# Two graph layers around an eigenvalue problem: one ScalarE table load, the first pair normed by batch, layer-0 work on both sides of a branch, a shorter norm

## The chip, the cores and the metric

The kernel runs on one core of one Trainium2 chip. The core has five engines that run on their own and meet at semaphores: TensorE (PE, matrix products into PSUM), ScalarE (ACT, functions and copies), VectorE (DVE, elementwise work and sums), GpSimd (POOL) and SyncE (SP), which here issues all the DMAs. The metric is the device time of one execution in microseconds, the lower the better.

## The reference

`x` is 64 matrices of 256 x 256 in float32. The result goes through two layers, each with a layer norm, a ReLU and a residual. Layer 0 multiplies by the squared adjacency matrix `adj * adj` three times, with weights of 256 x 512, 512 x 1024 and 1024 x 256. Layer 1 multiplies by the eigenvectors of a normalized Laplacian of the adjacency matrix.

```python
h = jnp.maximum(_layernorm(x, axis=-1), 0.0)
x = x + _L0_gnn_ref(h, adj, adj, W1, W2, W3)      # relu((adj*adj) @ (h @ W)), the last without relu
h = jnp.maximum(_layernorm(x, axis=-1), 0.0)
x = x + _L1_gnn_ref(h, adj, L1_W1, L1_b1, L1_W2, L1_b2)

# in _L1_gnn_ref
deg = jnp.sum(A, axis=0) + jnp.sum(A, axis=1) - jnp.diagonal(A)
L_norm = d_inv_sqrt[:, None] * (jnp.diag(deg) - A) * d_inv_sqrt[None, :]
_, U = jnp.linalg.eigh(L_norm)
agg = jnp.einsum('mn,bnd->bmd', U.T, features)
h = jax.nn.relu(agg @ W1 + b1)
return jnp.einsum('nm,bmd->bnd', U, h @ W2 + b2)
```

## The kernel before

There are two strands of work. The first is the eigenvalue problem, in the class `Eigen`: `laplacian` builds the matrix, `tridiagonalize` reduces it with 254 reflections, `leaves` solves blocks of 16 by steps on DVE, `level` merges blocks to 32, 64, 128 and 256, and `vectors` ends with the eigenvectors `u`, their transpose `ut`, and a flag that says whether anything went wrong on the quick way. This is a long chain of short instructions, most of them on DVE. In each reflection PE transposes two columns into rows (`psB`, `psA`), so DVE waits for PE and PE for DVE.

The second strand is layer 0 and the first half of layer 1, in the class `Layers`. It takes the 64 matrices in 32 pairs. `begin` loads a pair (`load`), norms it and writes `h0`; `first` multiplies by the squared adjacency `gt2`, `second` by W1 and `gt2`, `third` by W2, `fourth` by W3 in two halves, `last` by `gt2` and adds the residual to give `x1`. Then `norm1`, `turn_rows` and `for_layer1` give `hw`. `x1` and `hw` of all pairs but the last two are put into DRAM. Both strands need PE and ACT.

`Pace` sets the order in which the two strands stand on PE and ACT. It is written out while the program is built: `Pace` keeps a clock for each engine and a cost for each operation. `chain` issues an operation of the eigenvalue strand and, before it, lets `run` issue what the two generators of `Layers` (`products` and `rows`) have to offer and what by these costs can start earlier. Within an engine everything then runs in that order. For a small DVE operation the cost is 0.065 us plus one 960th of a microsecond for each element.

At the end of the eigenvalue strand `tile_kernel` calls `pace.go_on(FLAG_US)`, which issues so much more PE work by the planner's clock, and then `mend`. `mend` loads the flag into a register on every engine and branches: if the flag is set, the eigenvalues are done again by a slow way (with these inputs it is not set, and the branch jumps over that code). After it all engines meet. Then `layer1` fetches `hw` and `x1` of the first three pairs from DRAM (`fetch`), and in a loop over 32 pairs runs `to_vectors`, `from_vectors` and `finish`, in three stages that overlap. What is left of the second strand is mixed in until `pace.finish()` at turn 8.

The order at the front: SP issues `adj`, `ident`, `lower`, the two halves of the first pair (by rows, `h`), then the weights and the rest. The layer norm is in `norm`: four sums on ACT, the mean `nm` on DVE, four sums of squares on ACT, the variance `v`, a square root on ACT, one refining step of it on DVE, the reciprocal `scale` and the product `shift`; `relu_norm` then applies both with four ACT instructions. The profile's lines are nearly all line 191, in `issue`, since `Pace` makes the calls there; so one goes by the names of tiles.

Of the kernel before, what the change touches and what calls it, by code (L numbers as in the profile page):

```python
# [29 lines left out]
H = 2  # L30
PAIRS = 32
KEPT = 2
LAST_AT = 12
FLAG_US = 6.0
LN_EPS = 1e-5
EPS = 2.0**-24
BIG = 1.0e3
# [213 lines left out]
class Eigen:  # L251


    def __init__(self, tc, ctx, ap, gt2, pace):
        self.tc, self.nc, self.pace = tc, pace.now, pace
        self.gt2 = gt2
        self.ap = ap
        pool = ctx.enter_context(tc.tile_pool(name="eig_const", bufs=1))
        dma = tc.nc.sync.dma_start
        self.adj = pool.tile([P, H, N], F32, name="adj")  # L260
        dma(out=self.adj, in_=ap["adj"].rearrange("(h p) n -> p h n", p=P))
        mats = [pool.tile([P, H, N], F32, name=c) for c in ("ident", "lower", "upinc", "sub")]
        self.mats = mats
        self.ident, self.lower, self.upinc, self.sub = mats
        self.load_matrices(0, 2)
        self.iota, self.far, self.ones = (pool.tile([P, N], F32, name=c) for c in ("iota", "far", "ones"))
        tc.nc.vector.memset(self.ones, 1.0)
        self.cols = pool.tile([P, 1 + len(LEVELS), H], F32, name="cols")
        self.leaf = pool.tile([P, LEAF + 2], F32, name="leaf")
        self.mp = ctx.enter_context(tc.tile_pool(name="eig_mat", bufs=1))  # L270
        self.sp = ctx.enter_context(tc.tile_pool(name="eig_small", bufs=2))
        self.lp = ctx.enter_context(tc.tile_pool(name="eig_leaf", bufs=1))
        self.ps = ctx.enter_context(tc.tile_pool(name="eig_psum", bufs=1, space=PSUM))
# [1428 lines left out]
class Layers:  # L1702


    def __init__(self, tc, ctx, ap, gt2, u, ut):
        self.tc, self.nc, self.ap = tc, tc.nc, ap
        self.gt2, self.u, self.ut = gt2, u, ut
        pool = ctx.enter_context(tc.tile_pool(name="layers", bufs=1))
        self.kept = ctx.enter_context(tc.tile_pool(name="kept", bufs=KEPT))
        dram = ctx.enter_context(tc.tile_pool(name="dram", bufs=1, space=bass.MemoryType.DRAM))  # L1710
        self.x1, self.hw = {}, {}
        self.x, self.h0, self.y1, self.y2, self.s2, self.p3, self.h1, self.new = ({} for _ in range(8))
        self.begun = set()
# [24 lines left out]

    def load(self, q):
        self.x[q] = x = self.io.tile([P, H, 2, N], F32, tag="x", name="x")  # L1740
        for h in range(H):
            yield self.nc.sync.dma_start(out=x[:, h], in_=self.view(self.ap["x"], q)[:, h])

    def open(self, ctx):

# [29 lines left out]
        for i, (lhsT, rhs) in enumerate(pairs):  # L1775
            yield self.nc.tensor.matmul(out, lhsT=lhsT, rhs=rhs, start=i == 0, stop=i == len(pairs) - 1)

    def norm(self, x, scale, shift):

        nc = self.nc  # L1780
        g = H * 2
        s, nm, v, tmp = (self.sp.tile([P, g], F32, tag=c, name=c) for c in ("s", "nm", "v", "tmp"))
        for j in range(g):
            junk = self.sp.tile([P, N], F32, tag="junk", name="junk", bufs=1)
            yield nc.scalar.activation(junk, x[:, j // 2, j % 2, :], AF.Copy, accum_out=s[:, j : j + 1])
        yield nc.vector.tensor_scalar(nm, s, -1.0 / N, None, OP.mult)
        for j in range(g):
            junk = self.sp.tile([P, N], F32, tag="junk", name="junk", bufs=1)
            yield nc.scalar.activation(
                junk, x[:, j // 2, j % 2, :], AF.Square, bias=nm[:, j : j + 1], accum_out=v[:, j : j + 1]  # L1790
            )
        yield nc.vector.tensor_scalar(v, v, 1.0 / N, LN_EPS, OP.mult, OP.add)

        yield nc.scalar.activation(s, v, AF.Sqrt)
        yield nc.vector.reciprocal(tmp, s)
        yield nc.vector.tensor_tensor(tmp, tmp, v, OP.mult)
        yield nc.vector.tensor_tensor(s, s, tmp, OP.add)
        yield nc.vector.tensor_scalar(s, s, 0.5, None, OP.mult)
        yield nc.vector.reciprocal(scale, s)
        yield nc.vector.tensor_tensor(shift, nm, scale, OP.mult)  # L1800

    def relu_norm(self, x, scale, shift, tag):
        h = self.wp.tile([P, H, 2, N], F32, tag=tag, name=tag)
        for j in range(H * 2):
# [4 lines left out]
        return h  # L1809

    def project(self, rows, blocks, rhs, tag):

        out = self.wp.tile([P, blocks, 2 * N], F32, tag=tag, name=tag)
        for c in range(blocks):
            ps = self.bank()
            for b in range(2):
                yield from self.products_of(
                    ps[:, b * N : (b + 1) * N],
                    [(rows[:, h, b, c * P : (c + 1) * P], rhs[:, h, :]) for h in range(H)],
                )  # L1820
            yield self.nc.scalar.copy(out[:, c, :], ps)
        return out

    def streams(self):
        return Stream(self.products()), Stream(self.rows())
# [1 line left out]
    def products(self):  # L1827


        yield lambda: 0 in self.h0  # L1830
        yield from self.first(0)
        yield from self.second(0)
        for q in range(PAIRS):
# [6 lines left out]
            if q > 0:  # L1840
                yield from self.for_layer1(q - 1)
            if more:
                yield lambda: q + 1 in self.h0
                yield from self.first(q + 1)
            yield from self.fourth(q, 1)
            if more:
# [17 lines left out]
    def begin(self, q):  # L1864
# [73 lines left out]
    def norm1(self, q):  # L1938
# [4 lines left out]
        h1 = yield from self.relu_norm(x1, scale, shift, "h1")  # L1943
        self.h1[q] = h1

    def turn_rows(self, q):
# [100 lines left out]
    def layer1(self, pace):  # L2047
# [29 lines left out]
def tile_kernel(ctx: ExitStack, tc: tile.TileContext, ap):  # L2077
# [5 lines left out]
    with ExitStack() as inner:  # L2083
# [52 lines left out]
```

## Time and profile before

| | us |
|---|---|
| median of 3 runs | 2467.62 (2467.04 to 2468.11) |
| the profiled execution | 2468.13 |
| its span, from the first to the last instruction | 2466.3 |
| mean granted TensorE clock | 0.998 of full speed |
| ACT busy | 1011.8 |
| PE waits on `xr` of DVE | 69 times |
| the 64 loads of the input, from issue to landing | 3.7 (median) |

The chain of work that ended last goes back only to 2271.93, to SP's issue of the first fetch after the branch:

```profile
2271.93 0.02 SPq L191
2271.95 0.03 issue
2271.98 0.03 SPq L191
2272.01 0.04 issue
2272.05 3.01 DMA hw<-hw
2275.07 0.97 issue
2276.03 53.67 PE bank L191 x243
```

The columns are the start in us, the length in us, and the engine, tile and line. From 2276.03 on PE carries the chain to the end, but for a copy on ACT and the last addition on DVE. "issue" is time in which an engine waited for nothing that the profile shows. Before the branch the chain can't be followed, since all engines meet there; the stages before are read from busy times and waits.

A float32 product stands in the trace as two MATMUL records. Records of weight loads (PEld) run beside them.

### The profile page before, as it was taken

What the parts mean: (1) busy time and instruction counts of PE and PEld (TensorE: products, weight loads), DVE (VectorE), ACT (ScalarE), POOL (GpSimd) and SP (SyncE); (2) the same over time, 40 slices, a digit from 0 to 9 for tenths busy, and PEclk for the clock granted to TensorE, in tenths of its full rate; (3) what the DMA queues carried; (4) which work ended last, traced back from release to release, by engine and by line L of the source; (5) the groups of instructions that cost most, each with busy time, mean ns of one, the idle gap of its engine ahead of it and who ended that gap; (6) DMA issues with size and microseconds to landing.
All of it is one profiled execution on the core that took longest, in us unless ns stands there. A gap on an engine that the chain in (4) does not pass through costs nothing. (4 is left out here: it accounts for less than half of the span.)

```text
span 2466.3 us, 38232 instructions
## 1 busy us (share of the span) xinstructions
PE 2396.4 (97%) x8986; PEld 1546.4 (63%) x8986; DVE 2151.9 (87%) x13409; ACT 1011.8 (41%) x2826; POOL 476.8 (19%) x1625
## 2 busy tenths in 40 slices
PE   7999999999999999999999999999999999999999
PEld 4666655666655666655556666665566666665888
DVE  7999999999999999999999889998887888884333
ACT  4334444434444433444443244443444334443322
POOL 2333333333333111111111000000000000000343
PEclk9999999999999999999999999999999999999999
DMA  3000000000000000000000000000000000001476
GB/s 111 18 7 21 22 18 22 22 22 5 22 18 22 22 22 5 22 23 22 18 23 30 10 22 22 22 22 18 22 22 26 22 8 20 22 22 44 158 252 205
DMA packets 59400, 90.02 MB, mean 36 GB/s; under 512 B 5792, under 2 KB 42784, under 8 KB 59168
## 3 DMA queue, kind: packets, MB, share of 16 engines
q1 hardware_dynamic: 59168, 87.52, 10.8%
q8 instruction: 73, 1.20, 0.2%
q14 instruction: 159, 1.30, 0.2%
HBM read 47.13 MB, written 40.37 MB: 35 GB/s over the span
## 5 line engine op out<-in xcount | busy, mean ns | idle before, releaser
L191 PE MATMUL bank<-y,L_gnn_W 128*128 128x512 f32 x2048 | 905.4, 592 | 1.3 <-ACT y L191 1.3
L191 PEld LDWEIGHTS bank<-y,L_gnn_W 128*128 128x128 f32 x2048 | 379.1, 190 | 427.5 <-issue 409.9
L191 PE MATMUL bank<-L_gnn_W,s 128*128 128x256 f32 x2048 | 467.0, 381 | 2.4 <-ACT s L191 2.3
L191 PEld LDWEIGHTS bank<-L_gnn_W,s 128*128 128x128 f32 x2048 | 383.8, 191 | 52.7 <-ACT s L191 2.7
L191 ACT ACTIVATE s<-bank 128x512 f32<-128x512 f32 x384 | 224.7, 588 | 177.2 <-PE bank L191 176.0
L191 PE MATMUL bank<-gt,s 128*128 128x256 f32 x1024 | 230.3, 379 | 1.8 <-ACT s L191 1.8
L191 PE MATMUL bank<-L_gnn_W,y 128*128 128x512 f32 x512 | 228.8, 592 | 0.0
L191 PEld LDWEIGHTS bank<-gt,s 128*128 128x128 f32 x1024 | 192.0, 190 | 36.3 <-issue 9.8
L191 ACT ACTIVATE s<-nn,guard 128x1 f32<-128x1 f32 x254 | 75.0, 295 | 252.4 <-DVE nn L191 235.9
L191 POOL COPY m<-xr 128x1 f32<-128x1 f32 x254 | 56.0, 221 | 547.6 <-DVE xr L191 537.9
L191 ACT ACTIVATE h<-x,shift,scale 128x256 f32<-128x256 f32 x256 | 136.8, 593 | 58.3 <-DVE shift L191 58.2
L191 ACT COPY y<-bank 128x512 f32<-128x512 f32 x192 | 111.0, 582 | 114.7 <-PE bank L191 113.7
L191 PEld LDWEIGHTS bank<-L_gnn_W,y 128*128 128x128 f32 x512 | 95.2, 190 | 97.9 <-issue 90.6
L191 ACT ACTIVATE junk<-xr 128x254 f32<-128x254 f32 (+63 forms) x127 | 46.1, 363 | 264.1 <-DVE xr L191 263.7
L191 ACT ACTIVATE junk<-x,nm 128x256 f32<-128x256 f32 x256 | 129.6, 506 | 26.7 <-DVE nm L191 22.2
L191 DVE SCALAR_TENSOR_TENSOR A<-xr,wc,A 128x255 f32<-128x255 f32 (+63 forms) x381 | 139.9, 369 | 0.0
L191 ACT ACTIVATE junk<-x 128x256 f32<-128x256 f32 x256 | 105.9, 414 | 81.4 <-DVE x L191 66.7
L191 DVE SCALAR_TENSOR_TENSOR A<-wr,q,A 128x255 f32<-128x255 f32 (+63 forms) x381 | 139.1, 367 | 0.0
L191 PEld LDWEIGHTS psB<-ident,ac 128*128 128x128 f32 x381 | 44.7, 135 | 149.4 <-PE bank L191 76.7
L191 DVE SCALAR_TENSOR_TENSOR q<-q 128x1 f32<-128x1 f32 (+1 forms) x576 | 119.9, 209 | 16.4 <-ACT q L191 5.7
L191 PE MATMUL bank<-gt,h 128*128 128x256 f32 x512 | 119.9, 385 | 0.4 <-ACT h L191 0.4
L191 POOL TENSOR_TENSOR xb<-x,ub 128x512 f32<-128x512 f32 x16 | 19.9, 1271 | 516.0 <-DMA hw<-hw 491.5
(615 smaller groups left out, 4455.9 us busy)
## 6 DMA issues: line engine op xcount, KB each, us to landing
x<-x SPq DMA_DIRECT2D x60, 512.0 KB, 3.6
x<-in_x_dram SPq DMA_DIRECT2D x64, 256.0 KB, 3.7
out_dram<-out SPq DMA_DIRECT2D x64, 256.0 KB, 2.2
hw<-hw SPq DMA_DIRECT2D x60, 256.0 KB, 2.7
L_gnn_W<-in_L_gnn_W_dram SPq DMA_DIRECT2D x1, 2048.0 KB, 10.2
L_gnn_W<-in_L_gnn_W_dram SPq DMA_DIRECT2D x1, 1024.0 KB, 12.7
L_gnn_W<-in_L_gnn_W_dram SPq DMA_DIRECT2D x1, 512.0 KB, 5.5
mask<-in_c_blk_dram SPq DMA_DIRECT2D x2, 256.0 KB, 2.6
```

The source lines that it names most:

```text
L191: return op.call(*op.args, **op.kwargs)
```

## The change

It has four parts.

- At the front one square root of one column is issued on ACT as soon as `ones` is set, into a tile that is overwritten later (`far`). Of the two table loads of ACT one remains. SP's queue has `adj`, `ident`, the first pair, and only then `lower`.
- The first pair is loaded by batch instead of by rows, and normed and scaled in two halves, batch 0 and then batch 1. `first` works by batch for every pair, waits for each half by itself (`rows_of`), and copies each batch out of PSUM. `project` is gone, its work is in `first`.
- `FLAG_US` goes from 6.0 to 3.5, and after the branch, behind the first fetches, `pace.go_on(LOAD_US)` issues 4.5 us of layer-0 work by the planner's clock before the loop begins.
- In `norm` the variance is scaled by a quarter (and so is the epsilon), so that the refining step yields the root itself, and the multiplication by 0.5 goes.

```diff
-FLAG_US = 6.0
+FLAG_US = 3.5
+LOAD_US = 4.5
...
-        self.load_matrices(0, 2)
+        self.load_matrices(0, 1)
         self.iota, self.far, self.ones = (pool.tile([P, N], F32, name=c) for c in ("iota", "far", "ones"))
         tc.nc.vector.memset(self.ones, 1.0)
+
+        self.nc.scalar.activation(self.far[:, 0:1], self.ones[:, 0:1], AF.Sqrt)
...
     def load(self, q):
         self.x[q] = x = self.io.tile([P, H, 2, N], F32, tag="x", name="x")
-        for h in range(H):
-            yield self.nc.sync.dma_start(out=x[:, h], in_=self.view(self.ap["x"], q)[:, h])
+        rows = self.view(self.ap["x"], q)
+        for i in range(2):
+            at = (slice(None), slice(None), i) if q == 0 else (slice(None), i)
+            yield self.nc.sync.dma_start(out=x[at], in_=rows[at])
...
-    def norm(self, x, scale, shift):
+    def norm(self, x, scale, shift, parts=range(4)):
...
-        yield nc.vector.tensor_scalar(v, v, 1.0 / N, LN_EPS, OP.mult, OP.add)
-
+        s, nm, v, tmp, scale, shift = (t[:, at] for t in (s, nm, v, tmp, scale, shift))
+
+        yield nc.vector.tensor_scalar(v, v, 0.25 / N, 0.25 * LN_EPS, OP.mult, OP.add)
         yield nc.scalar.activation(s, v, AF.Sqrt)
         yield nc.vector.reciprocal(tmp, s)
         yield nc.vector.tensor_tensor(tmp, tmp, v, OP.mult)
         yield nc.vector.tensor_tensor(s, s, tmp, OP.add)
-        yield nc.vector.tensor_scalar(s, s, 0.5, None, OP.mult)
         yield nc.vector.reciprocal(scale, s)
         yield nc.vector.tensor_tensor(shift, nm, scale, OP.mult)
...
-        yield lambda: 0 in self.h0
         yield from self.first(0)
...
             if more:
-                yield lambda: q + 1 in self.h0
                 yield from self.first(q + 1)
...
-        yield from self.norm(x, scale, shift)
-        h0 = yield from self.relu_norm(x, scale, shift, "h0")
-        self.h0[q] = h0
+        h0 = self.normed("h0")
+
+        for parts in [(0, 2), (1, 3)] if q == 0 else [range(4)]:
+            yield from self.norm(x, scale, shift, parts)
+            yield from self.relu_norm(x, scale, shift, h0, parts)
+            self.h0[q] = h0
+            self.rows_of[q] = self.rows_of.get(q, 0) + (1 if q == 0 else 2)
 
     def first(self, q):
-        self.y1[q] = yield from self.project(self.h0[q], N // P, self.gt2, "y1")
+
+        self.y1[q] = y1 = self.wp.tile([P, H, 2 * N], F32, tag="y1", name="y1")
+        for b in range(2):
+            yield lambda b=b: self.rows_of.get(q, 0) > b
+            h0, ps = self.h0[q], self.bank()
+            for c in range(H):
+                yield from self.products_of(
+                    ps[:, c * N : (c + 1) * N],
+                    [(h0[:, h, b, c * P : (c + 1) * P], self.gt2[:, h, :]) for h in range(H)],
+                )
+            yield self.nc.scalar.copy(
+                y1[:, :, b * N : (b + 1) * N], ps.rearrange("p (c n) -> p c n", c=H)
+            )
         self.begun.add(q)
...
         with self.tc.manual_schedule():
             self.turn()
+            pace.go_on(LOAD_US)
             for i in range(PAIRS + 2):
...
         layers.nc = pace.now
+        eigen.load_matrices(1, 2)
         layers.load_weights()
         eigen.load_rest()
```

More of the change, by code (lines that the diff above doesn't have):

```diff
@@ L1712, in __init__ @@
         self.x, self.h0, self.y1, self.y2, self.s2, self.p3, self.h1, self.new = ({} for _ in range(8))
-        self.begun = set()
+        self.begun, self.rows_of = set(), {}
         self.due = False
@@ L1776, in products_of @@
             yield self.nc.tensor.matmul(out, lhsT=lhsT, rhs=rhs, start=i == 0, stop=i == len(pairs) - 1)
-    def norm(self, x, scale, shift):
+    def norm(self, x, scale, shift, parts=range(4)):
         nc = self.nc
         g = H * 2
+        at = slice(parts[0], parts[-1] + 1, parts[1] - parts[0])
         s, nm, v, tmp = (self.sp.tile([P, g], F32, tag=c, name=c) for c in ("s", "nm", "v", "tmp"))
-        for j in range(g):
+        for j in parts:
             junk = self.sp.tile([P, N], F32, tag="junk", name="junk", bufs=1)
             yield nc.scalar.activation(junk, x[:, j // 2, j % 2, :], AF.Copy, accum_out=s[:, j : j + 1])
-        yield nc.vector.tensor_scalar(nm, s, -1.0 / N, None, OP.mult)
-        for j in range(g):
+        yield nc.vector.tensor_scalar(nm[:, at], s[:, at], -1.0 / N, None, OP.mult)
+        for j in parts:
             junk = self.sp.tile([P, N], F32, tag="junk", name="junk", bufs=1)
@@ L1797, in norm, with relu_norm @@
         yield nc.vector.tensor_tensor(s, s, tmp, OP.add)
-        yield nc.vector.tensor_scalar(s, s, 0.5, None, OP.mult)
         yield nc.vector.reciprocal(scale, s)
         yield nc.vector.tensor_tensor(shift, nm, scale, OP.mult)
-    def relu_norm(self, x, scale, shift, tag):
-        h = self.wp.tile([P, H, 2, N], F32, tag=tag, name=tag)
-        for j in range(H * 2):
+    def relu_norm(self, x, scale, shift, h, parts=range(4)):
+        for j in parts:
             at = (slice(None), j // 2, j % 2)
@@ L1808, in relu_norm, with normed @@
             )
[L1809 to L1822, printed above, removed]
+    def normed(self, tag):
+        return self.wp.tile([P, H, 2, N], F32, tag=tag, name=tag)
     def streams(self):
@@ L1942, in norm1 @@
         yield from self.norm(x1, scale, shift)
-        h1 = yield from self.relu_norm(x1, scale, shift, "h1")
+        h1 = self.normed("h1")
+        yield from self.relu_norm(x1, scale, shift, h1)
         self.h1[q] = h1
```

## The prediction

> **What bounds the kernel now.** I read the page's first two parts, then a table of busy time by stage, then the list of what TensorE waited for, then the order of time at the two places where those waits are longest.
>
> From the page, busy time by engine, and from the table by stage (stretch, its length, busy time of PE, its weight loads, DVE, ACT, POOL, the granted clock, DMA):
>
> ```profile
> PE 2396.4 (97%) x8986; PEld 1546.4 (63%) x8986; DVE 2151.9 (87%) x13409; ACT 1011.8 (41%) x2826; POOL 476.8 (19%) x1625
> ```
> ```profile
> 0.00:18.52 18.52, 3.82 (x10) 2.18 (x10) 9.24 (x56) 9.24 (x25) 0.20 (x4) 1.00 0.94 315
> 18.52:60.00 41.48, 40.20 (x128) 23.29 (x129) 36.43 (x181) 19.38 (x56) 15.33 (x48) 1.00 0.10 25
> 60.00:1275.00 1215.00, 1183.68 (x4464) 737.42 (x4463) 1174.76 (x7586) 527.62 (x1547) 362.21 (x1413) 1.00 0.06 19
> 1275.00:1800.00 525.00, 511.09 (x1826) 321.60 (x1825) 475.97 (x3693) 210.61 (x592) 19.13 (x96) 0.99 0.06 20
> 1800.00:2270.00 470.00, 469.48 (x1695) 298.96 (x1694) 383.44 (x1788) 196.70 (x518) 0.00 (x0) 1.00 0.06 19
> 2270.00:2332.00 62.00, 57.84 (x266) 48.60 (x265) 19.72 (x33) 17.77 (x41) 24.33 (x20) 0.97 0.57 191
> 2332.00:2466.00 134.00, 130.24 (x607) 114.39 (x605) 52.36 (x76) 30.43 (x50) 55.60 (x45) 1.00 0.66 214
> ```
>
> TensorE (PE) is the bound, and the change takes no matmul from it. So only PE's idle or slow time can be won. It is, by stage: 14.7 us before the first layer-0 product at 18.52; 1.3 to 60; 31.3 while the matrix is made tridiagonal (60 to 1275); 13.9 in the leaf blocks (1275 to 1800); 0.5 to 2270; 4.2 around the branch. The last stage, without gaps, has none to give. What PE waited for (total, times, longest):
>
> ```profile
> PE psB L191 <- DVE xr L191: 28.7, 69, 1.4
> PE psB L191 <- DMA ident<-in_c_mats_dram: 4.5, 1, 4.5
> PE psB L191 <- DVE m L191: 3.6, 1, 3.6
> PE bank L191 <- DMA hw<-hw: 3.4, 1, 3.4
> ```
>
> The 28.7 us are 69 small waits, each where the hand-planned PE order reached an eigenvector transpose before VectorE (DVE) had its operand. The single waits are places. First the branch, in order of time on PE, then the branch instruction of each engine, then PE's clock just after:
>
> ```profile
> 2267.77 4.87 PE L191 MATMUL bank<-L_gnn_W,s 128*128 128x256 f32 x20
> 2276.03 1.19 PE L191 MATMUL bank<-hw,u 128*128 128x256 f32 x2 [3.39 <-DMA hw<-hw]
> ```
> ```profile
> L1698 DVEq COMPARE_BRANCH  x1: 72/72/72, 2266.3 to 2266.3; - x1
> L1698 PEldq COMPARE_BRANCH  x1: 3347/3347/3347, 2268.4 to 2268.4; - x1
> L1698 DVEq EVENT_SEMAPHORE  x1: 21/21/21, 2269.4 to 2269.4; - x1
> L1698 PEldq EVENT_SEMAPHORE  x1: 51/51/51, 2271.9 to 2271.9; - x1
> ```
> ```profile
> 2276.03:2279.45 3.42, 3.42 (x8) 0.50 0.96 343
> 2279.45:2283.00 3.55, 3.55 (x19) 1.00 1.02 402
> ```
>
> PE is the last to pass, at 2271.9; only then may SP issue the fetch of `hw` (2272.05, on the order of time); PE has one layer-0 product left, runs dry at 2272.64 and waits until 2276.03. And when it starts again it runs at half clock for 3.41 us: 8 records instead of 19 in nearly the same length. The wait costs 3.4 and the clock 0.5 x 3.4 = 1.7 more.
>
> Second the front, on ACT and on PE:
>
> ```profile
> 9.96 1.28 ACT L191 ACT_TABLE_LOAD   x1
> ```
> ```profile
> 12.96 2.08 PE L191 MATMUL psC<-ident,c 128*128 128x256 f32 x4 [7.36 <-DVE c L191]
> 17.49 0.66 PE L191 MATMUL psB<-ident,xc 128*128 128x128 f32 x2 [2.45 <-DVE s L191]
> 18.52 5.67 PE L191 MATMUL bank<-gt,h 128*128 128x256 f32 x14 [0.38 <-ACT h L191]
> ```
>
> Fourteen records in 5.67 us are 0.41 each, against 0.216 in the stream of `W,s` above: PE is cold here.
>
> **What the Trainium skill says.** "TensorE: Matmul & The Clock Gate", Part 1: an idle PE is held at half clock, in free-running windows of 3413 ns. The trace agrees: 3.41 us at 0.50 after the wait of 3.39. "ScalarE: Activation LUTs", What ACT_TABLE_LOAD costs: about 1283 ns, and about 1380 ns more of drain. The trace has the 1.28; the drain it doesn't show (the next ACT instruction starts 1.29 after the load's start). "Runtime: NRT & Kernel Launch", Instruction fetch mechanics: a taken branch to a far target waits for a fetch of instructions. That fits DVE, silent for 3.1 us after its 72 ns branch, and PE's 3.35 us; the trace can't tell such a fetch from a drain of PE's queue.
>
> **The branch (FLAG_US, LOAD_US).** In the changed PE order, between the flag's sum and the branch stand 3 products of W2, 8 transposes and 2 products of W3, two records each but for the transposes. With the distances from start to start of such records in the trace that is 6 x 0.43 + 8 x 0.109 + 4 x 0.216 = 4.3 us. Before it was 2, 8 and 9: 1.7 + 0.9 + 3.9 = 6.5. The flag is there 0.66 us after its sum starts (2264.96 to 2265.62); loading it took PE 0.49, the branch 3.35: PE could pass 4.7 us after the sum, DVE passes at 4.5 (2269.4). The 4.3 us of work cover that to 0.3 or so, about the pause of 0.3 between two matmuls that the trace has there now. After the branch PE now has 12 products of W3, 24 x 0.216 = 5.2 us, before the first one that needs `hw`. From SP's issue to that product it took 2276.03 - 2272.05 = 4.0. Hidden, with 1 us to spare. Gain: 3.4 + 1.7 = **5.1 us**. Bounds: nothing lost beyond the old pause, at least 3 if 1 us of wait and a half-slow window stay. Late next: nothing before the 0.62 us wait for `h` at 2330, which stays.
>
> **The front.** The input's first batch takes the place of `lower` in SP's queue and lands at about 5.95 (`lower`: issued 1.75, 4.2 us) in place of 6.81; `lower` is used only at about 16. ACT's two sums take 0.96, so `m` is copied from 6.9 (was 7.77). The root of the degrees no longer waits for the tables: with DVE's 2.0 us from `m` it comes at 9.7 (was 11.25). Five small DVE steps of the norm slip between those of the degrees: `c` is ready at 11.65 (was 12.96, gain 1.3). PE's `psC`: 11.65 to 13.7. `h` of batch 0 has been made by 12.7, so the first layer-0 product follows at once, at 13.5 instead of 18.52: 8 records at the cold 0.427 end at 16.9, and `xc`'s transpose goes behind them, about 0.6 before its old time.
>
> But batch 1 is late. In ACT's new order its squares stand behind the copy of batch 0's `y` out of PSUM (17.1 to 17.7), then come two squares (to 18.9), the tail of the first reflection (to 19.5), the root at 19.5, six DVE steps of 0.2, and two Relus of 0.55: the next layer-0 product starts at about 21.3, after PE was idle from 17.6, and cold again or still. Before, by 21.3, PE had done 7 such records without pause; now 8. The gain is one record, 0.2 to 0.4 us, less perhaps 1 us for a clock that rises a window later than at 23.24, plus 1 if the unbroken stretch from 11.65 to 17.6 warms it early. I take **0.3 us**, from -1.5 to +2.5. The table load and the earlier eigenvalue path are worth little, since each eigen step meets PE in a fixed order, and a lead of DVE is spent waiting there.
>
> `first` by batch lets `second` start on one copy instead of two; for later pairs a `fourth` of 32 records stands between them, so that hides it: nothing.
>
> **A step less in the norm.** 64 instructions of 0.165 us go from DVE. In 60 to 1275 DVE is 97% busy and PE waits on it; some 34 norms lie there: at most 5.6 us. But the planner takes the step out of its own costs too (0.065 + 4/960 = 0.069 us by its formula) and so packs PE's work tighter by that; and where the step lay inside the latency of a dependent chain it cost nothing. Between 0 and 34 x 0.1 = 3.3; I take **1 us**.
>
> Since the whole order is planned anew, the 45 us of small waits between 60 and 1800 are drawn again, among them 2.25 and 3.55 us in the leaf stage, each followed by a slow window (clock 0.99 there). No reason gives this a sign; I allow 4 to 5 us either way.
>
> **Sum.** 5.1 + 0.3 + 1.0 = 6.4. The profiled execution took 2468.1 (span 2466.3, 1.8 around it); 2461.7. The median of the runs stands 0.5 lower, so 2461.2 against 2467.6.
>
> **Rivals.** About 0.2% (4.9 us) is what a measurement of this kernel can tell from no change.
> - *The plan gives it back.* The redrawn waits cost 2 to 6 us more, and the result is 2463 to 2470, about 2466. For: 45 us of waits nobody aimed at. Against: they come from the same costs and sum over a hundred.
> - *The front pays in full.* If PE warms before 17 and batch 1 is ready near 19, PE wins 3 us more, and the shorter norm its 3.3: 6.4 + 2.7 + 2.3 = 11.4, 2456. Against: ACT's order above.
> - *Slower: DVE's lag in the leaf blocks.* There no transpose brings plan and chain together, so DVE's lag behind the plan grows until PE stops. If the new order starts these blocks with PE further ahead, the waits of 13.9 us and their two slow windows (3.4) nearly double: +17 - 6.4 = 2478. It decides from 11.3 us of added idle on. Against: costs and chain are those of before.
> - *The branch isn't mended*, because the fetch waits for something later than PE: 2466. For: several semaphores are waited for there. Against: SP's issue follows PE's mark by 0.15 us.
>
> **How the numbers follow.** Forecast 0.50 (of it 0.06 inside 0.2%); plan gives it back or branch not mended 0.24 (same); front in full 0.17 (faster); slower rival 0.09. Faster 0.61, same 0.30, slower 0.09. The range, 2455.5 to 2468.5, takes in both ends of the front, of the norm and of the redrawn waits; outside are the slower rival and a corner of each of two others, some 0.18.
>
> **What would show it.** Right: no wait of PE on `hw` over 0.5 us and no half clock after the branch; one table load; the first layer-0 product near 13.5, an idle stretch of 3 to 4 us from about 17.6; PE idle of 60 to 1800 within 5 us of 45. Wrong: PE dry before the branch; batch 1 ready by 19; that idle below 38 or above 52.

## The result, and the profile after

| | before | after |
|---|---|---|
| median of 8 runs each, us | 2467.86 (2467.04 to 2469.01) | 2461.35 (2459.61 to 2462.02) |
| the profiled execution, us | 2468.13 | 2461.43 |
| its span, us | 2466.3 | 2459.6 |
| mean granted TensorE clock | 0.998 | 0.997 |

The changed kernel takes 0.9972 of the time before (95% interval 0.9961 to 0.9983): 6.5 us less, where 6.4 were forecast. That the sum fits says little yet, since it has four terms. So first the stages. The table by stage of the changed kernel has the same stretches as the one of before, up to its own end (stretch, its length, then busy time with the number of instructions in brackets of PE, its weight loads, DVE, ACT, POOL, then granted clock, DMA share, GB/s):

```profile
0.00:18.52 18.52, 6.13 (x18) 4.58 (x18) 9.96 (x61) 9.37 (x29) 1.10 (x6) 1.00 0.89 306
18.52:60.00 41.48, 38.71 (x120) 22.24 (x121) 37.58 (x187) 18.86 (x57) 15.24 (x49) 0.92 0.12 29
60.00:1275.00 1215.00, 1188.62 (x4475) 739.48 (x4474) 1175.48 (x7585) 527.88 (x1551) 361.24 (x1415) 1.00 0.06 19
1275.00:1800.00 525.00, 509.02 (x1823) 319.24 (x1822) 471.73 (x3639) 208.18 (x587) 18.05 (x92) 0.99 0.06 20
1800.00:2270.00 470.00, 469.58 (x1691) 298.93 (x1690) 382.86 (x1777) 195.86 (x517) 0.00 (x0) 1.00 0.06 19
2270.00:2332.00 62.00, 61.38 (x295) 52.63 (x295) 19.22 (x32) 20.19 (x44) 24.83 (x20) 1.00 0.53 187
```

Length less busy time of PE is PE's idle time. From 60 to 1275 it is now 26.4 (was 31.3). In the leaf blocks, 1275 to 1800, it is 16.0 (was 13.9), and around the branch 0.6 (was 4.2). At the front one stop moved: PE is idle for 12.4 us up to 18.52 (was 14.7) and for 2.8 up to 60 (was 1.3). The clock of 0.92 there is not all new: the column counts as full speed what lies ahead of a trace's first clock record, and that record comes at 23.24 us before and at 15.65 now. Before, PE was at half clock up to 23.24 too (0.41 us a record). Now it is so up to 15.65, and again from 19.06 to 25.89.

What PE waited for in the changed kernel, in all (total us, times, longest):

```profile
PE psB L192 <- DVE xr L192: 24.0, 67, 0.8
PE psC L192 <- DVE c L192: 6.0, 1, 6.0
PE psB L192 <- DVE m L192: 5.1, 1, 5.1
...
PE bank L192 <- DVE den L192: 3.8, 1, 3.8
```

No line names `hw` any more; `xr` has 24.0 in place of 28.7; `m`, one wait in the leaf blocks, has grown from 3.6 to 5.1; `den` is new. It is PE's stop ahead of batch 1. The weight load of the same product names `h` of ACT (4.00 us), so `den` is only the last thing that the profile saw finish.

The branch, in order of time on PE, and the branch and the next instruction of PE and DVE (count, duration in ns, start):

```profile
2262.64 0.28 PE L192 MATMUL psC<-bad,ones 128*128 128x1 f32 x2
2262.78 2.82 PE L192 MATMUL bank<-y,L_gnn_W 128*128 128x512 f32 x6
2265.44 1.04 PE L192 MATMUL bank<-eye,h 128*128 128x128 f32 x8
2266.31 6.70 PE L192 MATMUL bank<-L_gnn_W,s 128*128 128x256 f32 x28
2272.85 0.59 PE L192 MATMUL bank<-hw,u 128*128 128x256 f32 x2
```
```profile
L1701 PEldq COMPARE_BRANCH  x1: 369/369/369, 2263.9 to 2263.9; - x1
...
L1701 PEldq EVENT_SEMAPHORE  x1: 51/51/51, 2267.4 to 2267.4; - x1
...
L1701 DVEq EVENT_SEMAPHORE  x1: 21/21/21, 2267.5 to 2267.5; - x1
```

The sum that makes the flag (`psC<-bad,ones`) starts at 2262.64 and PE passes at 2267.4, 4.8 us later. Between the 28 records on `L_gnn_W,s` and the first product on `hw` no wait is shown (no bracket at the end of the line), where 3.39 us stood before. Records still follow each other at 0.216 us (two in 0.43), so the clock is full too. The chain of waits confirms it: it now goes back to 2267.45 and begins with PE itself, no longer with a transfer.

```profile
2267.45 0.04 issue
2267.49 55.55 PE bank L192 x259
```

The front, on PE and then on ACT:

```profile
11.63 2.07 PE L192 MATMUL psC<-ident,c 128*128 128x256 f32 x4 [5.99 <-DVE c L192]
13.50 2.96 PE L192 MATMUL bank<-gt,h 128*128 128x256 f32 x8
16.30 0.38 PE L192 MATMUL psB<-ident,xc 128*128 128x128 f32 x2
20.44 1.22 PE L192 MATMUL bank<-gt,h 128*128 128x256 f32 x2 [3.76 <-DVE den L192]
```
```profile
16.50 0.59 ACT L192 COPY y<-bank 128x512 f32<-128x512 f32 x1 [1.43 <-PE bank L192]
...
18.52 0.19 ACT L192 ACTIVATE s<-v 128x2 f32<-128x2 f32 x1
...
19.79 1.09 ACT L192 ACTIVATE h<-x,shift,scale 128x256 f32<-128x256 f32 x2 [0.57 <-DVE shift L192]
```

`psC` starts at 11.63 and layer 0 at 13.50. After eight records and one transpose PE stops until batch 1 is normed. On ACT the copy of `y`, then the second half's root, then the second half's `h` can be seen in the order that the prediction named. One table load of ACT is left, at 0.73.

Idle time per stage doesn't show where the lead over the kernel before comes and goes, since the stages shift. For that I took the start of the n-th record of a product into `bank` (layer 0, and at the end layer 1; each trace has 7,936) in both traces, and subtracted. Those products are the same in all these kernels. The experiments below are read with this clock too (us against the kernel before, negative is earlier):

| record, and its time before | after | branch alone | norm, planned anew | norm, same order | front alone | root alone |
|---|---|---|---|---|---|---|
| 65th, 41.4 | -1.0 | +0.2 | -1.7 | +0.3 | -1.0 | -1.0 |
| 901st, 317.7 | -1.7 | +0.1 | -2.3 | -0.6 | -3.2 | -1.1 |
| 2651st, 890.4 | -4.4 | -0.2 | -3.4 | -2.0 | -5.3 | -1.4 |
| 4901st, 1601.2 | -4.2 | -0.5 | -2.5 | -2.1 | -5.8 | -1.8 |
| 5151st, 1674.6 | -1.1 | -0.6 | +0.5 | -2.3 | -6.0 | -1.8 |
| 6901st, 2209.8 | -1.5 | -0.6 | +0.8 | -3.6 | -5.9 | -1.1 |
| 7151st, 2292.1 | -6.7 | -5.3 | +2.4 | -3.6 | -6.0 | -1.2 |

The changed kernel wins 4.4 us by 890, loses 3.1 between 1600 and 1675, in the leaf blocks, and wins 5.2 at the branch. That is not the course the prediction described, although it ends where the prediction ends.

Each column is a single trace, so it has scatter. e1_branch_only and e8_load_only have the instructions and the order of the kernel before up to the flag; yet they stand at +0.2 and +1.8 at the 65th record, and then drift by 0.8 and 0.3 up to the 6901st. At the end the traces differ from the medians by up to 2.2 us (e6_replan_b: -1.9 by the trace, +0.3 by the medians). So a lead at the front of under 2 us isn't told from scatter; the growth along a column is firmer, to about 0.8.

### The profile page after: what moved, and what is told of

Same layout as the page of the kernel before. It is cut to its first block, busy times and chain, and to the rows that moved or that the text cites. A ratio compares the mean times of both kernels' runs of the same rounds, so it can differ in the third digit from the quotient of the medians.

```text
span 2459.6 us, 38181 instructions
## 1 busy us (share of the span) xinstructions
PE 2397.0 (97%) x8986; PEld 1545.5 (63%) x8986; DVE 2147.1 (87%) x13352; ACT 1008.9 (41%) x2827; POOL 475.5 (19%) x1625
## 5 line engine op out<-in xcount | busy, mean ns | idle before, releaser
L192 POOL TENSOR_TENSOR xb<-x,ub 128x512 f32<-128x512 f32 x16 | 19.8, 1275 | 511.3 <-DMA hw<-hw 489.5
```

The costliest lines, as they stand in the source:

```text
L192: return op.call(*op.args, **op.kwargs)
```

## The experiments

Times are medians; ratios are to the kernel before on the same chip. e9_after_replan, e10_leaf_pace and e11_fill ran on another chip than the changed kernel; there the kernel before takes 2469.31, and e9_after_replan, which is close to the changed kernel, 2461.4.

**e1_branch_only.** The kernel before with the change of the branch alone.

```diff
-FLAG_US = 6.0
+FLAG_US = 3.5
+LOAD_US = 4.5
...
             self.turn()
+            pace.go_on(LOAD_US)
```

> Only FLAG_US 3.5 and LOAD_US 4.5 are changed against the kernel before; all that stands ahead of the flag keeps its order. Theory A (the branch gain is the wait of 3.4 us on hw plus half of a 3.4 us window at half clock): 5.1 us faster, ratio 0.9979, no wait of PE on hw and full clock after the branch. Rival B (the branch gives the wait alone, the clock is no loss): 3.4 us faster, ratio 0.9986. Rival C (the whole gain of 6.5 us was won here): 6.5 us faster, ratio 0.9974.

2463.24 against 2468.42, ratio 0.9979 (0.9972 to 0.9987): -5.2. The lead comes in one place, from -0.6 at the 6901st record to -5.3 at the 7151st. The wait on `hw` and the half clock behind it are both gone. The interval alone would also admit rival B's 3.4 and rival C's 6.5; it is the trace, with both terms gone in this one place, that speaks for theory A. A pause of 0.80 us at the branch is left in this order.

**e8_load_only.** Of the two numbers, only the second.

```diff
 FLAG_US = 6.0
+LOAD_US = 4.5
...
             self.turn()
+            pace.go_on(LOAD_US)
```

> The kernel before with LOAD_US 4.5 behind the branch and FLAG_US left at 6.0. Theory A (LOAD_US alone hides the fetch; FLAG_US 3.5 was enough to cover the branch and 6.0 is too): as fast as with both, 5.1 us faster, ratio 0.9979, PE passes the branch about 6.9 us after the flag's sum instead of 4.8. Rival B (the shorter FLAG_US is needed so that the fetch is issued earlier): a wait on hw of 1 to 2 us is left, 2 to 3.5 us faster.

2463.67, ratio 0.998 (0.9973 to 0.9987): -4.8. In order of time on PE around its branch:

```profile
2266.49 0.28 PE L192 MATMUL psC<-bad,ones 128*128 128x1 f32 x2
2266.64 1.96 PE L192 MATMUL bank<-y,L_gnn_W 128*128 128x512 f32 x4
2268.43 1.04 PE L192 MATMUL bank<-eye,h 128*128 128x128 f32 x8
2269.31 4.05 PE L192 MATMUL bank<-L_gnn_W,s 128*128 128x256 f32 x18
2273.62 3.26 PE L192 MATMUL bank<-L_gnn_W,s 128*128 128x256 f32 x14 [0.26 <-PEq L1699]
```

With the old `FLAG_US` PE passes 7.1 us after the flag's sum and not 4.8. It costs no more than the 0.26 us pause, and the records that now lie behind the branch cover the fetch. So the work behind the branch does it all; the shortening of what stands ahead of it can't be told from nothing (the two intervals overlap almost wholly).

**e2_norm_only.** The kernel before with the shorter norm alone; the planner sees one step less and plans anew.

```diff
-        yield nc.vector.tensor_scalar(v, v, 1.0 / N, LN_EPS, OP.mult, OP.add)
+        yield nc.vector.tensor_scalar(v, v, 0.25 / N, 0.25 * LN_EPS, OP.mult, OP.add)
...
-        yield nc.vector.tensor_scalar(s, s, 0.5, None, OP.mult)
```

> Only the norm's step less is changed against the kernel before, with the whole order planned anew. Theory A (a small real gain, and the redrawn waits of no fixed sign): -1 us, but anything within 4 to 5 us either way. Rival B (the drift of -3 to -4 us between 250 and 1275 us that the changed kernel shows comes from the shorter norm): PE's idle time from 60 to 1275 falls by about 3 to 5 us, and the time by 3 to 4 us, ratio 0.9986.

2469.88, ratio 1.0006 (0.9998 to 1.0014): +1.5. PE's idle time from 60 to 1275 is 30.7 us (was 31.3), so rival B is out. The kernel is 2.5 us ahead at the 4901st record, and behind at the 5151st. What PE waits for in the leaf blocks, 1275 to 1800, is in this kernel

```profile
PE psB L191 <- DVE m L191: 5.1, 1, 5.1
PE bank L191 <- ACT s L191: 4.4, 4, 1.6
PE psD L191 <- DVE rb L191: 2.3, 2, 1.5
```

and in the changed kernel, same window,

```profile
PE psB L192 <- DVE m L192: 5.1, 1, 5.1
PE bank L192 <- ACT s L192: 4.4, 4, 1.6
PE psD L192 <- DVE rb L192: 2.3, 2, 1.5
```

The three lines are equal to a tenth of a microsecond. PE's order, too, is the same in both from the 3900th to the 5500th record. So the loss of 3.1 us in the leaf blocks of the changed kernel is the one that comes with the shorter norm's new plan. What PE loses there is not the wait on `m`: that one ends at 1785.92 in the changed kernel, behind the records between which the 3.1 are lost (from 1601 to 1675 in the kernel before). Between these PE waits for ACT's `y` (1.22) and `s` (0.88), which stand in ACT's order behind a step of the leaf blocks, and for that step ACT waits for DVE. The first of the two places, in the changed kernel, on ACT and on PE:

```profile
1614.02 0.22 ACT L192 ACTIVATE q<-q 128x15 f32<-128x15 f32 x1 [6.75 <-DVE q L192]
1614.14 1.05 ACT L192 COPY y<-bank 128x512 f32<-128x512 f32 x2
```
```profile
1614.76 2.41 PE L192 MATMUL bank<-p,gt 128*128 128x512 f32 x5 [1.22 <-ACT y L192]
```

The kernel before lists no wait of PE from 1540 to 1675; ACT's wait for `q` at this place is 4.78. The two waits are 2.1 of the 3.1 (2.4 counted from the start of one record to that of the next); the rest is in smaller delays. Behind the 5151st record the waits of the two plans nearly balance. Both kernels have 6.83 us at half clock around the wait on `m`, where the kernel before has two windows of 3.41 in this stage; so the clock isn't what differs. A further 1.6 us are lost at the branch, where this kernel has a pause of 0.82, its wait on `hw` is 3.8 (was 3.4), and the half clock behind it lasts 6.83 us (was 3.41), of which the first 2.2 still lie in the wait.

**e3_norm_same_order.** The same arithmetic, but the planner still counts the step that isn't issued, so every engine's order is that of the kernel before.

```diff
-        yield nc.vector.tensor_scalar(s, s, 0.5, None, OP.mult)
+        halved = nc.vector.tensor_scalar(s, s, 0.5, None, OP.mult)
+        halved.call = lambda *args, **kwargs: None
+        yield halved
```

> The norm's step is planned but not issued: PE, ACT and POOL keep the order of the kernel before to the instruction, DVE's order lacks 64 steps. So it has the price of the step without a new plan. Theory A (the step lies mostly in the latency of other chains): 0 to 3 us faster, about -1. Rival B (DVE decides from 60 to 1275, each step there counts in full): 34 x 0.165 = 5.6 us faster, ratio 0.9977. In both nothing can get slower.

2464.72, ratio 0.9986 (0.9979 to 0.9993): -3.7. The lead grows slowly, from -0.6 at 317 to -2.0 at 890 and -3.6 at 2210. That is above theory A's 3 and below rival B's 5.6. So the step is worth 3.6 us by itself, and it is the new plan that gives 5 us back.

**e4_front_only.** The kernel before with the front of the change: root, `lower` later, the first pair by batch, `first` by batch. Norm and branch are those of before.

```diff
-        self.load_matrices(0, 2)
+        self.load_matrices(0, 1)
...
+        self.nc.scalar.activation(self.far[:, 0:1], self.ones[:, 0:1], AF.Sqrt)
...
+        for parts in [(0, 2), (1, 3)] if q == 0 else [range(4)]:
+            yield from self.norm(x, scale, shift, parts)
+            yield from self.relu_norm(x, scale, shift, h0, parts)
```

> Only the front is changed against the kernel before: the early root, lower behind the input, the first pair by batch; FLAG_US 6.0, no LOAD_US, the old norm. Theory A (the front itself gives nothing by the 16th layer-0 record, a new plan follows): within 1 us up to 100 us of the trace, and then the redrawn waits, 4 to 5 us either way. Rival B (the front pays): 2 to 4 us faster, and already there by 60 us.

2463.0, ratio 0.9979 (0.9973 to 0.9986): -5.4. The prediction had -0.3 for the front, and theory A 4 to 5 us either way for the redrawn waits. Up to the 65th record it is -1.0. The rest comes later, where no instruction of the front is left: -3.2 at 317, -5.3 at 890.

**e7_first_by_batch.** To see whether that drift is from `first`, which runs for all 32 pairs: only `first` written by batch, with one copy a batch.

```diff
-        self.y1[q] = yield from self.project(self.h0[q], N // P, self.gt2, "y1")
+        for b in range(2):
+            yield lambda: q in self.h0
+            h0, ps = self.h0[q], self.bank()
...
+            yield self.nc.scalar.copy(
+                y1[:, :, b * N : (b + 1) * N], ps.rearrange("p (c n) -> p c n", c=H)
+            )
```

> The kernel before with only the method first as in the changed kernel, batch by batch in every pair, waiting for the whole pair: PE's order of groups is that of the kernel before, one copy of each pair comes out of PSUM by batch. Theory A (hidden behind fourth): within 1 us of the kernel before. Rival B (this is what gives the front change its drift of -4 us): 3 to 5 us faster, ratio 0.9984, with less idle of PE from 60 to 800.

2468.02, ratio 0.9999 (0.999 to 1.0007): nothing, as forecast.

**e12_root_only.** To see whether it is from the eigenvalue strand standing earlier: only the root and `lower`.

```diff
-        self.load_matrices(0, 2)
+        self.load_matrices(0, 1)
...
+        self.nc.scalar.activation(self.far[:, 0:1], self.ones[:, 0:1], AF.Sqrt)
...
+        eigen.load_matrices(1, 2)
         layers.load_weights()
```

> The kernel before with two edits at the front alone: the early square root of one column on ACT, and lower behind the first pair in SP's queue. The first pair is still loaded by rows, normed whole and multiplied as before; norm, FLAG and the branch are those of before. e4_front_only, which adds to this the loading, norm and product of the first pair by batch, gave -5.4 us, of which only 1 stood at the 64th layer-0 record and 4 came later, between 150 and 900 us. Theory A (the later gain comes from the eigenvalue strand standing earlier by the table load, about 1.3 us at its first steps): psC about 1.3 us earlier, one table load, layer-0 records of the first 100 us within 1 us of before, then a gain that grows between 150 and 900 us to 4 to 5 in all: 2462.5 to 2464.5 against 2468, and PE idle of 60 to 800 falls from 19.4 to about 15. Theory B (it needs the batches: layer 0 starting at 13.5 and then being held up, which puts PE later against its plan): -0.3 to -1.5 us, 2466 to 2467.5, no growth after 150 us, PE idle of 60 to 800 stays 18 to 20. In between (-2 to -3): both have a share, or the drift is particular to each redrawn order.

2466.52, ratio 0.9993 (0.9985 to 1.0001): -1.8 by the medians, with an interval that takes in no change, and -1.2 in the traces. The order of the two strands on PE is exactly that of before. `psC` starts at 11.30, 1.66 us earlier than before. 0.7 of it is spent by 25 us, the rest stays: the lead is -1.0 from 25 us to 230 and then creeps to -1.8 by 1675. The time and the missing growth are those of theory B. PE's waits on `xr` from 60 to 800 are, in the kernel before, with the root alone, and with the whole front:

```profile
PE psB L191 <- DVE xr L191: 16.8, 41, 1.4
```
```profile
PE psB L191 <- DVE xr L191: 16.6, 41, 1.4
```
```profile
PE psB L191 <- DVE xr L191: 12.5, 34, 1.4
```

With the root alone the waits stay; they shrink once the first pair goes by batch as well, which also redraws the plan. The batches don't suffice for it, as the next run shows.

**e11_fill.** If the batches help and PE then stops for 3.8 us, that stop should be worth filling: the changed kernel with `second`'s product by W1 split by batch as well, so that W1's half for batch 0 stands in the gap.

```diff
-        yield from self.first(0)
+        yield from self.first(0, [0])
+        yield from self.widen(0, [0])
+        yield from self.first(0, [1])
+        yield from self.widen(0, [1])
```

> The changed kernel with the first pair's product by W1 taken batch by batch too: batch 0's four products by W1 stand ahead of batch 1's products by gt2 on PE. Theory (PE's stop from 16.7 to 20.4 us and the cold windows after it are what the front gave away): PE has those 8 records of 0.43 us done in the stop, does not fall to half clock, and is 3 to 5 us ahead of the changed kernel at the 64th layer-0 record; in total 2456 to 2459 if the redrawn waits stay. Rival (ACT, which has two more Relus to do there, delays batch 1 by as much): under 1.5 us ahead at that record.

2460.61, ratio 0.9967 (0.9954 to 0.9979): -0.8 against the changed kernel and against e9_after_replan, so the 2456 to 2459 of the theory were missed. The gap was filled, in order of time on PE:

```profile
16.97 3.70 PE L192 MATMUL bank<-L_gnn_W,y 128*128 128x512 f32 x8 [0.33 <-ACT y L192]
20.51 0.38 PE L192 MATMUL psB<-ident,ac 128*128 128x128 f32 x2
```

At the 65th record this kernel is 4.3 us ahead of the changed one, still 4.6 at the 901st, then 2.2 at the 2651st and 0.9 at the end. PE's idle time from 60 to 800 is 19.3 us, that of the kernel before (19.45), and not the 15.0 of the changed kernel. Against the kernel before it keeps the lead of the front, 5.3 us at the 65th record and 6.6 at the 2651st. What it lacks is the growth of 3.4 us that the changed kernel has between these records, and so most of the advantage is gone.

**e5_replan_a, e6_replan_b.** How much does a new plan alone move the time? The kernel before with the planner's factor `SLOWER` of the eigenvalue strand at 1.0605 (below) and at 1.062 in place of 1.06.

```diff
-    SLOWER, IN_BLOCKS = 1.06, 1.13
+    SLOWER, IN_BLOCKS = 1.0605, 1.13
```

> The kernel before with one number of the planner changed: SLOWER from 1.06 to 1.0605, which changes no instruction and only the order on PE and ACT. Theory A (a redrawn plan alone moves the time by some us, in the waits from 60 to 1800): between 2463 and 2473, and another value than the kernel before by over 1.5 us. Rival B (the drift of -4 us from 250 to 900 us with the front's change is a thing of its instructions): within 1 us of the kernel before.

> As the run before with SLOWER 1.062, a second draw. Theory A: again 2463 to 2473, and not the same as the first draw. Rival B: within 1 us of the kernel before. A third possibility: both are faster by a similar amount, since the planner then leaves DVE a little more time; then PE's idle from 60 to 1275 falls in both.

The first: 2471.24, ratio 1.0011 (1.0004 to 1.0018), +2.8, of which 3.5 arise in the leaf blocks. There PE's longest wait on `m` is 4.8 us. The second: 2468.71, ratio 1.0 (0.9992 to 1.0008), +0.3. But the order on PE hardly changed up to about 880 us: of the first 600 PE instructions of the eigenvalue strand 44 and 52 have another number of layer-0 records ahead of them (262 in e4_front_only). So they tell how the leaf blocks are redrawn, and little of the tridiagonal stage. The first loses in the leaf blocks what the shorter norm's plan loses there, although here the planner counts the eigenvalue strand slower and not shorter.

**e9_after_replan.** The same edit on the changed kernel, `SLOWER` 1.0605, to see whether its smaller waits before 800 were luck of its plan.

> The changed kernel with SLOWER 1.0605, so the same instructions in a redrawn order. Theory A (the -4 us of drift that the front change brought between 250 and 900 us was a lucky draw of the plan): 1 to 5 us slower than the changed kernel, 2462 to 2466, with PE's idle from 60 to 1275 back at 28 to 31 us. Rival B (it comes with the front's instructions, whatever the plan): PE's idle there stays at 25 to 27 us, and what changes lies after 1300 us.

2461.4, ratio 0.9971 (0.9958 to 0.9983): as the changed kernel. Here too only 44 of the 600 have moved, none ahead of 420 us, so it doesn't answer the question.

**e10_leaf_pace.** In the leaf blocks DVE falls behind the plan. The changed kernel, with the planner's factor for these blocks at 1.16 in place of 1.13, so that PE gets more layer-0 work ahead of each step:

```diff
-    SLOWER, IN_BLOCKS = 1.06, 1.13
+    SLOWER, IN_BLOCKS = 1.06, 1.16
```

> The changed kernel with IN_BLOCKS 1.16 for 1.13: the planner counts DVE's chain in the leaf blocks 2.7 percent slower and puts more layer-0 work between. Theory (DVE's lag behind the plan in the leaf blocks is what stops PE there, and the lag is 2 to 3 percent): PE's idle from 1275 to 1800 falls from 16 to under 8 us, the slow windows at 1784 vanish (3.4 us more), 8 to 11 us faster than the changed kernel, about 2451. Rival (the waits there are of single places, not of a lag): within 3 us of 2461.

2452.48, ratio 0.9932 (0.9919 to 0.9946): 16.8 us less than before, 8.9 less than the changed kernel, and the fastest of all. The line of the table by stage for the leaf blocks, 1275 to 1800, and PE's wait on `m` there:

```profile
1275.00:1800.00 525.00, 516.23 (x1867) 327.57 (x1866) 469.85 (x3629) 210.26 (x588) 17.86 (x92) 1.00 0.06 20
```
```profile
PE psB L192 <- DVE m L192: 1.7, 1, 1.7
```

PE is idle for 8.8 us there and not 16.0; the wait on `m` falls from 5.1 to 1.7, and one half-clock window of 3.41 us stands behind it and not 6.83. ACT's waits for `q` of DVE in this stage fall from 84.8 to 60.5 us. The idle time is 7.2 of the 8.9. The clock is some 0.6 more: the first 2.2 us of the 6.83 lay in the wait, so that 4.7 us of work at half clock stand against 3.4. Some 1 us isn't traced. The size and the place are those of the theory (8 to 11 us), the idle time is a little above its 8, and the slow windows were halved and not gone.

## Why the prediction came out right, step by step

**The branch: right in mechanism and size.** 5.1 forecast, 5.2 in the changed kernel (from the 6901st to the 7151st record) and 5.2 for the part alone (by its medians; 4.7 between these records of its trace, where the pause of 0.80 is left). Both terms held: the wait of 3.4 and the 1.7 that the half clock cost. "Could pass 4.7 us after the sum" measured 4.8, although the three terms named for it add up to 4.5. What the prediction left unsaid is that one of the two numbers suffices (e8_load_only).

**The front: what it described came true, what it concluded was wrong.** `psC` at 11.65, the first product at 13.5 and batch 1 at 21.3 were forecast; 11.63, 13.50 and 20.44 were measured. Its 8 records ended at 16.5 and not at 16.9, since PE reached full clock at 15.65, and fell back to half clock within its stop, from 19.06 to 25.89. The lead at the 65th record is 1.0, inside the bounds. The step that failed is "a lead of DVE is spent waiting there". In an unchanged order an offset set at the front stays: the lead of 1.0 of e12_root_only at 25 us is 1.1 at the 6901st record, and the 1.8 by which the trace of e8_load_only is late at the 65th are still 1.5. With the front alone the lead even grew from 1.0 to 5.8 us by 1600, while PE waited 4.3 us less on `xr` between 60 and 800. Neither `first` by batch (0) nor the earlier root (1.2) brings that growth; it is there when the first pair goes by batch together with them, and no run separates the batches from the order that the planner then draws. Why it grows is only partly settled. In the changed kernel and in e4_front_only, behind the first transposes, PE's fixed order has up to 8 layer-0 records fewer ahead of an eigenvalue step than in the kernel before, up to about 450 us, and no steady shortfall after. So the eigenvalue strand was let ahead of layer 0, and the layer-0 work put off could come where PE had waited. Filling PE's stop instead (e11_fill) put 2 to 16 more records ahead up to about 310 us, and the waits were those of before. That fits one reading, which no run tests by itself: over the tridiagonal stage DVE's chain sets the pace, and layer-0 work done at the front is missing later, where PE waits in its place. It doesn't show whether any plan that starts layer 0 so would gain as much, or just this one; the runs that were to redraw the plan left that stretch nearly as it was. (The waits on `xr`, which the prediction puts down to eigenvector transposes in a hand-planned order, are those of the reflections' transposes: 66 of the 69 lie between 60 and 1275, and the order is the one that `Pace` computes.)

**The norm: under-sized as a step, and taken back by its plan.** The step was taken at 1.0, between 0 and 3.3. (By the trace 32 norms lie between 60 and 1275, not 34.) In an unchanged order it is worth 3.6 by the traces. Half of that, 1.8, is there by 1294, within the bounds. The other half comes in the leaf blocks and after, up to 2210, where the prediction counted no norm at all. But with the plan that follows from it, it made the kernel 1.5 us slower. The prediction allowed 4 to 5 us either way for redrawn waits and found no reason for a sign. e2_norm_only shows that the loss of 3.1 us in the leaf blocks comes with this edit: the changed kernel takes over its waits there line by line. That a step less in the costs must lose there isn't shown; e5_replan_a, whose costs moved the other way, loses 3.5 at the same place, and e6_replan_b loses nothing. The mechanism of the slower rival, DVE's lag behind the plan in the leaf blocks, was there all the same, at a fifth of the price that was put on it. e10_leaf_pace, which gives DVE more time in the plan, confirms it from the other side. It runs through ACT as well as through PE, which the prediction didn't say: ACT waits for DVE in its fixed order, and layer 0 for ACT.

**The sum was right by offsets.** In the terms of the prediction: branch 5.1 and measured 5.2; front, norm and redrawn waits together 1.3 and measured 1.5 (the lead at the 6901st record), made of 4.2 won by 1600, 3.1 lost in the leaf blocks and 0.4 won after. The parts also don't add. Alone they give -5.2, -5.4 and +1.5, in all -9.1, against -6.5. At the 4901st record, ahead of most of the leaf loss, branch, front and norm have -0.5, -5.8 and -2.5, and the changed kernel has -4.2 and not -8.8. Front and norm both win before 1275 from waits of PE on DVE, so it may be that the second finds little left; this is a reading and not shown. The half clock at the front doesn't explain it: it lasts 6.83 us in the changed kernel and 3.41 in e4_front_only, but the first is at full clock from 15.65 and the second only from 17.49, and at the 65th record both lead by 1.0. The shortfall is a difference between runs whose plans differ, and no run takes it apart. That the terms offset each other to within 0.2 us of the forecast is luck.

**What would show it.** PE idle of 60 to 1800 was to stay within 5 us of 45: it is 42.4. Neither "PE dry before the branch" nor "batch 1 ready by 19" came about.

## What to carry to other kernels

Where an engine's order is planned from costs, an edit is worth its time in the old order plus what the new plan does; the two are measured apart by leaving the cost in the plan and the instruction out of the program. Behind a branch at which all engines meet, have work queued that needs nothing fetched after it, for as long as the fetch takes (here 4.0 us from its issue to the first product that needs it, covered by 5.2 us of work). When the total fits, subtract the starts of the same records in both traces all the same: here the sum was right while three of its terms were not.

## What the runs showed of the hardware

**The length of PE's branch isn't its price.** Before, PE's branch instruction stood in the trace with 3347 ns, and in the changed kernel with 369. Yet from its start to PE's next instruction it took 3.5 us in both (2268.4 to 2271.9, and 2263.9 to 2267.4). DVE, with 72 ns, was silent for 3.1 and 3.5 us, POOL, with 45 ns, for 0.5 and 0.4. In the changed kernel PE's sequencer met the branch at 2263.9, while its queued matmuls of before the branch ran on for some 3 us, so most of the 3.5 us cost nothing. In the prediction I left open whether these 3 us are a fetch or a drain of PE's queue. In e1_branch_only PE's queue was empty 0.8 us before PE went on, 3.7 us after its branch had begun (the bracket names PE's own sequencer):

```profile
2267.18 1.89 PE L192 MATMUL bank<-L_gnn_W,s 128*128 128x256 f32 x8
2269.88 5.42 PE L192 MATMUL bank<-L_gnn_W,s 128*128 128x256 f32 x24 [0.80 <-PEq L1699]
```

A drain of the queue alone would have ended there. This speaks for the fetch that the Trainium skill names ("Runtime: NRT & Kernel Launch", Instruction fetch mechanics). The page gives no time for it; here, in six traces (before, changed, e1, e2, e8, e10), it is 2.9 to 3.7 us on PE and DVE. Why POOL is through in 0.5, no run shows.

**Half clock comes in whole windows on a fixed grid, and where a wait falls decides.** The Trainium skill ("TensorE: Matmul & The Clock Gate", Part 1) has an idle window of about 3.4 us ahead of the half clock. Here less sufficed, but not always. The same wait of 2.2 to 2.3 us for ACT's `s` near 1720 stands in eight traces. In the kernel before and in e3_norm_same_order a half-clock window follows it, at 1723.08 in the kernel before; in e1, e4, e6, e7, e8 and e12 none does. In the kernel before, and in e4_front_only:

```profile
1721.63 4.97 PE L191 MATMUL bank<-L_gnn_W,s 128*128 128x256 f32 x14 [2.25 <-ACT s L191]
```
```profile
1715.72 4.15 PE L191 MATMUL bank<-L_gnn_W,s 128*128 128x256 f32 x18 [2.25 <-ACT s L191]
```

The clock records of each trace lie on a grid of 3.413 us. In the kernel before the first is at 23.24, and half clock begins at 1723.08, 1787.93 and 2276.03: 498, 19 and 143 steps apart. The idle time of PE within one step of this grid, worked out from the PE records of the fourteen traces up to 2440 us, tells the two cases apart. In all 27 full-clock steps with 1.97 us of it or more, half clock followed. Of the others, with up to 1.95, it followed one (1.72, in e10_leaf_pace). The wait in the kernel before has 1.97 us within one step, that in e4_front_only 1.81. A half-clock step was followed by another when PE was idle for 0.75 us or more in it, and by full clock with 0.50 or less; that is how 6.83 us come about. So in this kernel a wait of 2 us or more may cost half of each half-clock window behind it, less the part that the wait itself covers: 1.7 us for the wait on `hw` in the kernel before, and by this estimate 2.7 and 2.3 for the two of 6.83 in the changed kernel, of which 1.38 and 2.17 lie in the wait.
